# A two-layer model kernel: loads, table, TensorE and step order of the lead-in changed

## The chip, the cores and the metric

The kernel runs on one core of a Trainium2 chip. The metric is the device time of one execution in microseconds (us). A core has the engines PE (TensorE, matmuls and transposes), DVE (VectorE), ACT (ScalarE), POOL (GpSimd) and SP (SyncE), each with its own instruction queue that is worked off in order. DMA loads are issued from the queues of SP, ACT and POOL.

## The reference, cut to what matters

All numbers are float32. There are 2 x 1024 tokens of 256 channels, in 16 tiles of 128 tokens. Layer 0 normalizes the rows, runs grouped attention over 16 query heads of 16 channels with rotary positions, and gates its result with a feed-forward network whose weights are entries of a table of 16 numbers. Layer 1 does the same with a recurrent attention and a mixture of eight experts.

```
xn = layernorm(x)
s  = attention(xn)                       # q, k, v, rope, softmax, W_O
g  = silu(down(silu(gate(xn)) * up(xn))) # weights lut[idx]
x  = x + s * g
xn = layernorm(x)
s  = recurrent_attention(xn, Wx, Ww, bw, Wk, Wv, Wr, Wout, gamma, beta)
g  = silu(shared_experts(xn) + top_2_of_8_experts(xn))
x  = x + s * g
```

The change touches the start of layer 0 above all: layer norm, q, k, v, the first scores.

## The kernel before

The kernel is cut into small steps, and a step is a Python function that issues a few instructions on several engines. The string `ORDER` (L78 to L100), 1982 letters long, says in which order the steps are issued: each letter takes the next step of its kind. No scheduler moves anything afterwards, so the string sets the order of every engine's queue and, for DMA loads that a step issues, of the load queues as well. Semaphores hold an instruction until its operands are there.

Steps of layer 0 that the text speaks of, with the letter in front:

- `a`, `stats(t)`, for two tiles of tokens: two `bn_stats` and two `bn_aggr` on DVE, a root on ACT (L162), a reciprocal on DVE (L163) and, for the first sequence (tiles 0 to 7), a product on DVE (L167). At tile 8 it also clears the second sequence's buffers on POOL.
- `b`, `norm(t)`: one tile normalized, on ACT (L179) in the first sequence and on DVE (L181) in the second.
- `e`, `turn_x(t)`: four transposes on PE (L189) for two tiles, and one copy on ACT (L192).
- `f`, `qkv(t)`: one 128x512 product on PE over two halves of the channels (L200), the rotary products `cs` on DVE (L205), the values' copy on ACT (L211).
- `g`, `rotate(t)`: four operations on POOL (L223, L226) which finish q and k.
- `h`, `turn_k(t)` and `j`, `l`, turns of q: transposes on PE (L237, L269, L279) and a copy on ACT each.
- `m`, `largest`: one score product `mx` of 32 rows by 512 on PE (L291) and its maximum on DVE (L298), 512 times.
- `w`, `weigh`: the score product `sc` (L314, L322) and its exponential on ACT (L326), 512 times. `v`, `gather`: the weighted values `cx` (L339, L350).
- `z`, `decode`: one of 16 rounds over one of 8 pieces of the feed-forward weights on POOL (L252, L256). The first round of a piece issues its `idx` load on SP (L248).
- `W`: the product of two decay weights from `fold`, which lies in the buffer of `s_sb` (L603). `A`: gate, up and down products of layer 0 (L539, L555).
- From `>` on come the steps of layer 1; among them `r` (recurrence), `o` (routing), `F X G H D S` (experts), `k u U` (collecting and writing out).

Ahead of the steps stand the loads: x in seven pieces, taken in turn by SP and ACT; `cst` (identity and other constants), `lut` and `wo` on POOL; `wqkv`, `rope` and, last, `fold` on ACT. PSUM is one pool of eight banks of 128x512 in layer 0.

Of the kernel before, what the change touches and what calls it, by code (L numbers as in the profile page):

```python
# [12 lines left out]
F32 = mybir.dt.float32  # L13
I32 = mybir.dt.int32
AF = mybir.ActivationFunctionType
# [3 lines left out]
P = 128  # L19
# [3 lines left out]
NTC = NT // P  # L23
CPB = S // P
E = 256
KC = E // P
XLOADS = ((0, 1), (1, 2), (2, 4), (4, 6), (6, 8), (8, 12), (12, 16))
NBLK = NT // 512
BC = 512 // P
EPS = 1e-5  # L30
# [45 lines left out]


ORDER = """  # L78
aaabbbabeazbebfgefgfgbzbbbfgehfgeffghgfjfhmmgmhmmgmmmmmmjfmmmlWmwmzmmwwwmmwlmmwmmwzmwwmwmmzwmmwm
wmwwmwmmmmljmmmzzwwmmvmmzmwvmzwmmmmlvmmmmvmmwwzwmwmzmwmwmwzmwmwgmzwmwwmmmmlvvazmwmmmwzwbvvmwzwmw  # L80
mwmmwmwmwmwjbmwzwmmmzzwweyhwmmwmmwmvwmzmmvzwwmmfmwwmvwmwgmmwwzavwmmmmwwvvwmwlvazvwmmmmwwfmmwwwwm
jzmmmwwzmwwmwzwmmmwzwmwvmwgmmmwzwvmwmwmwwmwmwwmzmmmlyvwmmmvmwwmvwmzwmvbwzmmzwvwzmmbwvwwmmwwmmhez
wwmmjmwwmbmmwwvwwmmvmmwwwwmvmmwmwwwvwwwmmmlfyjwwbmzwvzmwzmwvwwmmvmwwmvwwmmwmmwfmwwmeywwmmzwmzzmw
mwwzmgwzzmmfmmmmwmwvvwwmmzzwwvmmgmwwwmvwmmzwmvwmmwvmmwgmlfwwwmzvwzwmmvwmwmzmmwwjywmmwwzmmwgwmmmz
wzhwmwwwmmzvwmwmwmmvvwwzwzmmmwvmwmwwmwvmmzwmjlvwzwzmwmmwvmwwwmmmzvhwwmwmzmwzzzzzwmmwmwwzmmwwmmww
mwmmvwwzmwzmmvwzmwwmwmvwmmmwzwzwvylwwmmwmzvmmmwwwvmmmmwwwzvvzwmwzzmzmzwmwjmzwwmmwzwwywmwzwmwmmvm
zzwmzmppzjvzzmmzwwwwwvzmwwzwlvmwmmvwmwwmwvmmmwwwzmvvwmmwwmwzmqmmwwwwmmqwwmzmwmzzwmvmmwwvwwmmmmmv
vmmmwwzmpylwwmmwmvwmwwmmwvwzwwwwzmmzvwwwmmwzmvwmmmmwwwqpwmmwwmwzmzjwmmmmwmmpqmmwwvvwmmwjpvmzwwmv
wwwwqzy<pzqlwzmwmvmwmwmwwvmwmmwmwvwmwmwmvmwmwmwmwqmwmwzwmwwmwmmwmmwmwpwmwmmwmvvwmmmwmmvwwwmvzvzw
mmmzAAmwwmjlymwwmmzmmvwmmmwwvzzzvmwmmwwmwmwmwwwmmwwwmwvwwwwwwmvvwmwmmwmAwmmwAmmzwwyAzlmwwmAjmmmw  # L90
AAmmmwvzvwwwmmmwvmwmmmzwwvwwmmmwmvwzwwmmmwmvwmwmmwwvwwwwvzwwwwvvzwwmmqylmwmwvwmmwvwwmwwmmvmzwmmw
wwmmwmwwwwmwmwmwyAmmmmAmmmmAzjmwwwvvmmwmzvmmwwvwmwmwmmvlmwwwmmwvwwwwmmwzvwwwwmmmvmwwmmmwwwmwmwww
mmmwwmmmwmwmwvwmmwvvmwwmwmmvzwmwwwwzylvwzwwwwwwvvwwwwvvwwwwvwwwwyAvvwwwwApwwwwAAqwwwwvvwwwwpAvvp
AqypAqAqAApAApqpAAqqpAAq>nniAAAnAAAiAAAAniAiAnoiAiAnoAAoAnAnrrrAAoiAnAAoArAsAAcAAAiAcnonArncsAii
nrsoincr)onssnrosooossoosoocioiooorsocoocsoosooooroooioooooooooiioooorroooiooorroorrr]FXFFciXFiG
GXrHcXGiFHXFFGDFSrHXFDHGciXrDDcSGXrHHcGDFSGXXFSDFSHGrHSXFDHGSXGcDrHDXFFDcSHGGSFSXFDHXiHGrDSXFDHr
FrDSSGXGrrHXrFrFSrHDGXGcXDSHGFHGSDXrFSFHDXDcGHGXDiHXFFGirSHGFSiDHSDcSXDSHrFXDcFGrcSGXHFiHXGDGSFX
DHXrcSHDGXDGHFFXGHXSGDFXSrHcDFHGGSFXSXFrSDDHGSHDGSFSXDHrrHiGXSDDrFGXHrrSSrDrHSGDrHcDSSckrdkkuukU
ukrdkUkucUurciUkkiuUUkurckduUrcdcurUkukUkuUrrUdukurUkrduUUuuUU
"""  # L100


def attention(nc, tc, st, b0, small, singles, xs, xnT, s_sb, wlut, ident, epst, wqkv_d, rope_d, lut_d, idx_d, wo_d):

# [2 lines left out]
    att = st.enter_context(tc.tile_pool(name="att", bufs=1))  # L109
# [4 lines left out]

    wqkv = att.tile([P, KC, 512], F32, name="wqkv")
    nc.scalar.dma_start(wqkv, wqkv_d)
    rope = att.tile([P, 2, CPB, 8], F32, name="rope")
    nc.scalar.dma_start(rope, rope_d)
    lut = att.tile([P, LUT], F32, name="lut")
    nc.gpsimd.dma_start(lut, lut_d)  # L120
    wo = att.tile([P, KC, E], F32, name="wo")
    nc.gpsimd.dma_start(wo, wo_d)


    knat = [att.tile([P, KV, SLOT], F32, name=f"knat{k}") for k in range(4)]
# [12 lines left out]
    def clear(b):  # L138
        nc.gpsimd.memset(vpads[b][:, :, :, HD : HD + 1], 1.0)
        nc.gpsimd.memset(vpads[b][:, :, 0, 0 : SLOT - HP], 0.0)  # L140
        nc.gpsimd.memset(vpf[b][:, NV * HP :], 0.0)
        for T in range(NQT):
            nc.gpsimd.memset(qns[b][:, T, :, :, HD:], 0.0)

    clear(0)

    def values(b, c, k):
        at = (c * KV + k) * HP
        return vpf[b][:, at : at + SLOT]


    mvs, rstds = {}, {}

    def stats(t):

        mv = att.tile([P, 2, 2], F32, name=f"mv_a{t}")
        for k in range(2):
            bst = att2.tile([P, 6], F32, tag="bst", name=f"bst_a{t + k}", bufs=4)
            nc.vector.bn_stats(bst, xs[:, t + k, :])
            nc.vector.bn_aggr(mv[:, k, :], bst)  # L160
        rstd = att.tile([P, 2], F32, name=f"rstd_a{t}")
        nc.scalar.activation(rstd, mv[:, :, 1], AF.Sqrt, bias=epst)  # L162
        nc.vector.reciprocal(rstd, rstd)  # L163
        if t == CPB:
            clear(1)
        if t < CPB:
            nc.vector.scalar_tensor_tensor(  # L167
                mv[:, :, 0], mv[:, :, 0], -1.0, rstd, ALU.mult, ALU.mult
            )
        for k in range(2):  # L170
            mvs[t + k] = mv[:, k, 0:1]
            rstds[t + k] = rstd[:, k : k + 1]
# [224 lines left out]
    def each(f, *ranges):  # L397
        return [lambda a=a: f(*a) for a in itertools.product(*ranges)]

    return {  # L400
        "a": each(stats, range(0, NTC, 2)),
        "b": each(norm, range(NTC)),
        "e": each(turn_x, range(0, NTC, 2)),
        "f": each(qkv, range(NTC)),
# [15 lines left out]
def two_layer_kernel(  # L420
# [22 lines left out]
    nc = tc.nc  # L443
    ctx.enter_context(tc.manual_schedule())
    pers = ctx.enter_context(tc.tile_pool(name="pers", bufs=1))
    small = ctx.enter_context(tc.tile_pool(name="small", bufs=2))
# [14 lines left out]
    xs = pers.tile([P, NTC, E], F32, name="xs")  # L461
    x_v = x_d.rearrange("(c p) e -> p c e", p=P)
    for n, (lo, hi) in enumerate(XLOADS):
        (nc.sync, nc.scalar)[n % 2].dma_start(xs[:, lo:hi, :], x_v[:, lo:hi, :])
    cst = pers.tile([P, C_ALL], F32, name="cst")
    nc.gpsimd.dma_start(cst, cst_d)
    ident = cst[:, C_ID : C_ID + P]
    before = cst[:, C_BEF : C_BEF + P]
    cols = cst[:, C_COL : C_COL + P]
# [3 lines left out]
    epst = pers.tile([P, 1], F32, name="epst")  # L473
    nc.vector.memset(epst, EPS)
    xnT = pers.tile([P, KC, NT], F32, name="xnT")
    s_sb = pers.tile([P, NTC, E], F32, name="s_sb")
    wxw = pers.tile([P, KC, E], F32, name="wxw")

# [19 lines left out]
    singles = []  # L498
    ffw = ctx.enter_context(ExitStack())
    wpool = ffw.enter_context(tc.tile_pool(name="ffw", bufs=1, side="right"))  # L500
    wlut = wpool.tile([P, WLUT], F32, name="wlut")
# [49 lines left out]
    def down0(n, k):  # L551
# [19 lines left out]
    b0 = seq0.enter_context(tc.tile_pool(name="b0", bufs=1, side="right"))  # L571
    att = ExitStack()
    singles.append(att.enter_context(tc.tile_pool(name="one", bufs=8, space=psum)))
    steps = attention(
        nc, tc, att, b0, small, singles, xs, xnT, s_sb, wlut, ident, epst,
        wqkv_d, rope_d, lut_d, idx_d, wo_d,
    )

    def end_sequence0():
# [6 lines left out]
    def go(last):  # L586
        for letter in order:
            if letter == last:
                break
            steps[letter].pop(0)()  # L590


    fold = s_sb.rearrange("p c e -> p (c e)")[:, 0 : 2 * KC * E].rearrange(
        "p (k f d) -> p k f d", k=KC, d=E
    )
    nc.scalar.dma_start(fold, fold_d)

    def weights_of_decays():
        ps = bank1("wxwp")
# [755 lines left out]
    def each(f, *ranges):  # L1355
        return [lambda a=a: f(*a) for a in itertools.product(*ranges)]
# [150 lines left out]
```

## Time and profile before

| | |
|---|---|
| median of 3 runs | 985.89 us (985.19 to 987.99) |
| profiled execution | 988.5 us, its span 986.7 us |
| busy: PE, DVE, ACT, POOL | 950.2, 631.3, 533.9, 587.9 us |
| first matmul on PE | 11.08 us after the span's start |
| first `mx` | 34.88 us |
| last decoding on POOL | about 493 us |

Times in a timeline count from the span's start. "x4" is a count of instructions; PE records a float32 product as two matmuls. PE counts as busy while any matmul is in flight, so a busy PE can still be at less than its best. In a line of the waits, the engine and line in front waited for the one behind the arrow.

### The profile page before, as it was taken

The numbers are of one execution on the slowest core, as the hardware profiler recorded it, in microseconds if no ns is written. First come the engines' busy times: TensorE is split into PE (matmuls) and PEld (weight loads), VectorE is DVE, ScalarE is ACT, GpSimd is POOL, SyncE is SP. The second block draws the span as 40 slices with busy tenths as digits, with TensorE's granted clock in tenths as the row PEclk, the third lists the DMA queues.
The fourth block names the chain that finished last, engine by engine and source line by source line (L and its number), as shares of the span: only waits on it lengthen the run. The fifth ranks groups of instructions, "written<-read, shape, count | busy, mean of one in ns | idle before, by whom it ended". The sixth has DMA issues, their size and how long they took to land.

```text
span 986.7 us, 17241 instructions
## 1 busy us (share of the span) xinstructions
PE 950.2 (96%) x6708; PEld 519.8 (53%) x6708; DVE 631.3 (64%) x1226; ACT 533.9 (54%) x1007; POOL 587.9 (60%) x483
## 2 busy tenths in 40 slices
PE   5999999999999999999999999999999999999965
PEld 2587343333433434333345474756457777767754
DVE  4799887877878767676770132767776625631893
ACT  3347766556665666677578535326433453563131
POOL 6999999999999999999901120302002454454232
PEclk9999999999999999999999999999999999999988
DMA  5000000000000000000000040102600122121242
GB/s 173 2 2 13 2 1 12 2 12 2 12 1 2 12 1 12 2 1 1 1 1 1 1 137 4 44 1 68 195 1 28 54 66 65 58 77 55 73 137 70
DMA packets 17960, 34.53 MB, mean 35 GB/s; under 512 B 2877, under 2 KB 11343, under 8 KB 17535
## 3 DMA queue, kind: packets, MB, share of 16 engines
q1 hardware_dynamic: 12583, 20.65, 6.5%
q0 software_dynamic: 3920, 10.74, 3.5%
q10 hardware_dynamic: 1376, 2.03, 0.6%
q8 instruction: 54, 0.88, 0.4%
q14 instruction: 27, 0.22, 0.1%
HBM read 22.01 MB, written 11.40 MB: 34 GB/s over the span
## 4 chain that ended last, share of the span: by engine, by line
PE 88%; DVE 6%; DMA 2%; ACT 1%; issue 1%; POOL 1%; POOLq 0%; ACTq 0%; SPq 0%; DVEq 0%
PE sc L322 14%; PE mx L291 14%; PE cx L350 12%; PE gu L539 7%; PE gus L723 4%; PE d L555 4%; PE gue L963 4%; PE dne L991 3%; PE qkv L200 3%; PE lev L1201 2%; DVE top L298 2%; PE so L392 2%; PE sc L314 1%; PE s L1324 1%; PE kp L1105 1%; PE rp L1105 1%
## 5 line engine op out<-in xcount | busy, mean ns | idle before, releaser
L298 DVE TENSOR_REDUCE top<-mx 128x1 f32<-128x512 f32 x512 | 324.8, 683 | 91.9 <-PE mx L291 64.2
L326 ACT ACTIVATE e<-sc 128x512 f32<-128x512 f32 x512 | 272.8, 600 | 130.1 <-PE sc L322 61.0
L291 PE MATMUL mx<-kT,qTa 32*128 32x512 f32 x1024 | 279.4, 625 | 0.0
L252 POOL TENSOR_SCALAR pick<-idx,lut 128x544 f32<-128x544 int32 x120 | 252.3, 2102 | 11.2
L322 PE MATMUL sc<-qTb,kT 32*128 32x512 f32 x960 | 258.3, 625 | 0.0
L256 POOL TENSOR_TENSOR wlut<-wlut,pick 128x544 f32<-128x544 f32 x120 | 160.8, 1340 | 10.0
L291 PEld LDWEIGHTS mx<-kT,qTa 32*128 32x128 f32 x1024 | 102.1, 183 | 66.5 <-DVE top L298 28.3
L322 PEld LDWEIGHTS sc<-qTb,kT 32*128 32x128 f32 x960 | 89.8, 183 | 79.9 <-DVE top L298 28.1
L350 PE MATMUL cx<-e,vpad 128*32 128x512 f32 x960 | 123.5, 602 | 0.0
L565 POOL TENSOR_TENSOR sgt<-s_sb,g 128x256 f32<-128x256 f32 x16 | 13.1, 816 | 158.2 <-ACT g L563 158.2
L936 POOL DMA_INDIRECT xg<-xn_h,who x39 | 39.7, 1017 | 102.4 <-ACT s_sb L1331 71.4
L1004 POOL DMA_INDIRECT y_h<-ye,who x39 | 39.9, 1023 | 63.0 <-ACT ye L999 16.9
L539 PE MATMUL gu<-xnT,wlut 128*128 128x512 f32 x160 | 73.3, 598 | 0.0
L350 PEld LDWEIGHTS cx<-e,vpad 128*32 128x32 f32 x960 | 21.1, 108 | 83.0 <-issue 71.6
L549 DVE TENSOR_TENSOR h<-sg,gu 128x512 f32<-128x512 f32 x20 | 13.8, 688 | 70.9 <-ACT sg L548 54.8
L975 DVE TENSOR_TENSOR sge<-sge,gue 128x176 f32<-128x176 f32 x39 | 13.1, 338 | 62.9 <-ACT sge L974 62.7
L963 PE MATMUL gue<-wgu,xT 128*128 x156 | 52.3, 460 | 0.6 <-DVE w L1239 0.6
L539 PEld LDWEIGHTS gu<-xnT,wlut 128*128 128x128 f32 x160 | 29.0, 190 | 33.7 <-issue 29.5
L555 PE MATMUL d<-wlut,h 128*128 128x256 f32 x192 | 43.6, 381 | 0.5 <-ACT s_sb L395 0.5
L723 PE MATMUL gus<-xnT,wgs 128*128 128x512 f32 (+1 forms) x96 | 43.4, 598 | 0.5 <-ACT aT L1116 0.5
L1208 DVE TENSOR_TENSOR rd<-rd,up 128x512 f32<-128x512 f32 x48 | 33.2, 733 | 16.1 <-PE lev L1201 16.0
L555 PEld LDWEIGHTS d<-wlut,h 128*128 128x128 f32 x192 | 36.0, 190 | 8.7 <-issue 2.7
(226 smaller groups left out, 1349.7 us busy)
## 6 DMA issues: line engine op xcount, KB each, us to landing
xn_h<-xn SPq DMA_DIRECT2D x16, 256.0 KB, 3.3
yk<-y_h SPq DMA_DIRECT2D x16, 256.0 KB, 2.9
wgu<-in_wgu SPq DMA_DIRECT2D x1, 2816.0 KB, 9.9
idx<-in_idx SPq DMA_DIRECT2D x8, 272.0 KB, 2.7
out_x<-g SPq DMA_DIRECT2D x16, 128.0 KB, 1.7
wd<-in_wd SPq DMA_DIRECT2D x1, 1408.0 KB
w<-in_w SPq DMA_DIRECT2D x1, 1024.0 KB
wgs<-in_wgs SPq DMA_DIRECT2D x1, 704.0 KB
```

Source lines behind the costliest of these rows:

```text
L252: nc.gpsimd.tensor_scalar(dst, codes[piece], float(j), lut[:, j : j + 1], ALU.is_equal, ALU.mult)
L256: nc.gpsimd.tensor_tensor(wlut[:, at], wlut[:, at], dst, ALU.add)
L291: nc.tensor.matmul(ps, qTs["qTa", g, c // BC][at, ts(c % BC, P)], kTs[b][at, T // 2, ts(half, 512)], start=True, stop=True,)
L298: nc.vector.tensor_reduce(tops[g, c][:, half, i : i + 1], ps, AX.X, ALU.max)
L322: nc.tensor.matmul(ps, kTs[b][at, T // 2, ts(c, P)], qTs["qTb", g, h][at, :], start=True, stop=True)
L326: nc.scalar.activation(e, ps, AF.Exp, scale=1.0 / math.sqrt(E))
L350: nc.tensor.matmul(cxs[g, h][SLOT * i : SLOT * (i + 1), :], values(b, c, 4 * (T // 2) + i), es.pop((n, i)), start=(c == 0), stop=(c == CPB ...
L539: nc.tensor.matmul(hT0[which], wlut[:, lo + kc * P :][:, 0:P], xnT[:, kc, ts(n, 512)], start=(kc == 0), stop=(kc == KC - 1),)
L555: nc.tensor.matmul(po[:, 0:E], hidden(n)[:, f, ts(k, P)], wd0[:, f, :], start=(f == 0), stop=(f == NF0 - 1),)
L723: nc.tensor.matmul(ps[:sz, which, :], wgs[:, kc, which * SH_CH + lo : which * SH_CH + lo + sz], xnT[:, kc, ts(n, 512)], start=(kc == 0), s ...
L963: nc.tensor.matmul(ps[:, 0 : 2 * EI], xT[:, kc, :], late["gu"][:, kc, bass.ds(e * (2 * EI), 2 * EI)], start=(kc == 0), stop=(kc == KC - 1),)
L1004: nc.gpsimd.indirect_dma_start(out=y_h[:, :], out_offset=bass.IndirectOffsetOnAxis(ap=who[:, i : i + 1], axis=0), in_=tiles.pop(("y", i))[ ...
```

## The change

- The loads of x for tiles 8 to 15 and of `fold` no longer stand in front. They are issued on SP from the third `scales` step; a small DVE write into those tiles of x, in the same step, is what the loads of x wait for. Of `cst` only the identity is loaded at first; the rest and `wo` follow on POOL after the first clearing of buffers. `rope` goes from ACT's queue to POOL's. Of the five pieces of x left, ACT issues one and SP four.
- ACT takes one root of a constant right after its two load issues, which brings its table.
- `stats` ends with the root. The reciprocal and the product are a step of their own, `scales`, letter `t`.
- PE multiplies a zeroed part of `xnT` with itself four times into four banks that nobody reads, at the very start. DVE writes the zeros.
- `ORDER` is another string, of 1990 letters: the eight `t` are new, all other letters are as many as before. Its start:

```
before aaabbbabeazbebfgefgfgbzbbbfgehfgeffghgfjfhmmgmhmmgmmmmmmjfmmmlWmwmz
after  atbbazeatbbtafbetgfgbafegtbbbfhgbfegffgjhfemgmgmzmhhazWmmmmmmmjfltfm
```

Counted in the string before, letters 298 to 459 are the same in both (eight places later in the new one), and nearly the same up to about letter 930. After that the two differ all the way to the end.

```diff
-XLOADS = ((0, 1), (1, 2), (2, 4), (4, 6), (6, 8), (8, 12), (12, 16))
+XLOADS = ((0, 1), (1, 2), (2, 4), (4, 6), (6, 8))
...
     wqkv = att.tile([P, KC, 512], F32, name="wqkv")
     nc.scalar.dma_start(wqkv, wqkv_d)
+    nc.scalar.activation(att.tile([P, 1], F32, name="root"), epst, AF.Sqrt)
     rope = att.tile([P, 2, CPB, 8], F32, name="rope")
-    nc.scalar.dma_start(rope, rope_d)
+    nc.gpsimd.dma_start(rope, rope_d)
...
-    nc.gpsimd.dma_start(wo, wo_d)
+    for k in range(4):
+        nc.tensor.matmul(bank(f"none_{k}"), xnT[:, 0, 0:P], xnT[:, 0, 0:512], start=True, stop=True)
...
     clear(0)
+    late_loads(0)
+    nc.gpsimd.dma_start(wo, wo_d)
...
         nc.scalar.activation(rstd, mv[:, :, 1], AF.Sqrt, bias=epst)
-        nc.vector.reciprocal(rstd, rstd)
         if t == CPB:
             clear(1)
+        mvs[t], rstds[t] = mv, rstd
+
+    def scales(t):
+        mv, rstd = mvs[t], rstds[t]
+        nc.vector.reciprocal(rstd, rstd)
+        if t == BC:
+            nc.vector.memset(xs[:, CPB:, 0:1], 0.0)
+            late_loads(1)
         if t < CPB:
             nc.vector.scalar_tensor_tensor(
...
-        (nc.sync, nc.scalar)[n % 2].dma_start(xs[:, lo:hi, :], x_v[:, lo:hi, :])
+        (nc.sync, nc.scalar)[n == 1].dma_start(xs[:, lo:hi, :], x_v[:, lo:hi, :])
...
-    nc.gpsimd.dma_start(cst, cst_d)
+    nc.gpsimd.dma_start(cst[:, 0:P], cst_d[:, 0:P])
...
+    nc.vector.memset(xnT[:, 0, 0:512], 0.0)
...
+    def late_loads(part):
+        if part == 0:
+            nc.gpsimd.dma_start(cst[:, P:], cst_d[:, P:])
+            return
+        for lo in range(CPB, NTC, 4):
+            nc.sync.dma_start(xs[:, lo : lo + 4, :], x_v[:, lo : lo + 4, :])
+        nc.sync.dma_start(fold, fold_d)
...
-    nc.scalar.dma_start(fold, fold_d)
```

More of the change, by code (lines that the diff above doesn't have):

```diff
@@ L78 @@
 ORDER = """
[L79 to L99, printed above, removed]
-"""
-def attention(nc, tc, st, b0, small, singles, xs, xnT, s_sb, wlut, ident, epst, wqkv_d, rope_d, lut_d, idx_d, wo_d):
+atbbazeatbbtafbetgfgbafegtbbbfhgbfegffgjhfemgmgmzmhhazWmmmmmmmjfltfmmmmwmwwmmwmwmmwmmmlwmmmwzwmw
@@ new lines @@
+wmwmmmgwzlmmwmmwmwwmwmmwmwmzmgwzvmmmmvvbmmmwmmwjlmwzmzmzwbwmwmmwmzwzvmmmwmmzwvmzmmmvemmwlmmmmmwm
+vvwmwmwmwmwmwwmwmmwwmwhmmwwmmwvwmmwvwwmmmwjzzmzwmwwwmvzwmmmwwzmazvfvwmmzwmtzwwvvalymtwgmmfzmwwzz
+wvmmmwjwwmwmwmmwwmwmwzwmmmwzwmwvmwgmmmwzwvmwmwmwwmwmwwmzmmmlyvwmmmvmwwmvwmzwmvbwzmmzwvwzmmbwvwwm
+mwwmmhezwwmmjmwwmbmmwwvwwmmvmmwwwwmvmmwmwwwvwwwmmmlfyjwwbmzwvzmwzmwvwwmmvmwwmvwwmmwmzmwfmwzwmeyw
+wmmwmzzmwmwwmgwzmmfmzmmmwmwvvwmwmwwvmzmmwwwgmvwmmzwmvwmmwvmmwgmlfwwwmzvwzwmmvwmzmwmzmwwjywmzmwzw
+mmwgwmmmzwhwmwwwmmvzwmwmwmmvvwwwzzmmmwvmwmwwmwvmmzwmjlvwzwzmwmmwvmwwwmmmzvhwwmwmzmwzzzzzwmmwmwwz
@@ new lines @@
+mmwwmmwwmwmmvwwzmwzmmvwzmwwmwmvwmmmwzwzwvylwwmmwmzvmmmwwwvmmmmwwwzvvzwmwzzmzmzwmwjmzwwmmwzwwywmw
+zwmwmmvmmzzwzmppzjvzzmmzwwwwwvzmwwzwlvmwmmvwmwwmwvmmmwwwzmvvmwwmmwwzmqmmwwwwmmqwwmzmwmzzwmvmmwwv
+wmmmmwmvvmmmwwzmpylwwmmwmvwmwwwmmvwzwwwwmmzvwwwmzmwzmvwmmmmwwwqpwmmwwmwzmzjwmzwmwmmwypqpwmmmwmmm
+vvqwmwmvzzmwmmmmjlqpwwwwwwmvvwmwwwwmvzwzzmmwvwwzmmvwzw<mmmwwmpqwwmmwwmmmwmwwwmmmwmwwzvvmmmwmmwvw
+mmmvwwwmjAmwmmlAwwmmvvwmwmwmmvymmmmmwvwwmwmmwmwwmwwmwwwmmwwwmmzwmwwmmmwwmwvvwwmmyzlAAwwmmzvmmwwv
+wwmwwmmvAmwmmvvwwwmvAAAwmmmwmwjwmmwmwmwwmwwwmmmwwmmmwmmzwwvvwwwmwwmvjwwwmvwmzzmmlyAzwwwmvmmwmzvA
@@ new lines @@
+mwwwwzmvvwwmmwwwmwwmmwmmwwwmmzwmmmmwwwwzvmmmmwwwvwmwwmmwvwwwmyAlmmmmvvmmwmqzwwmmvvmwwwmmmvmwwwmm
+mwzwmwzwmwwmwwmwwmwmwvmwmwwmwvwmzmmwmwvwzwwwzlyvvwwwwwwwvvvwwwwwwwwvAvAwwwwyApApqvwwwwvAwwwwvAAw
+wwwvwwwvAAvpqApAqyApAqpAqqpApqAq>nAnAnAAAAAiAAiAAniAnAAioAniiAnArrnriAAniAAAicAAAArAAAriAocAoion
+osAnAnonioinnorsnocsoio)oscsoorsosioosrooososooooroooosooococsooorooocooooooroooroioooiorr]FrrXr
+FFGcXXFFiHGXGrHXDFcGHFGSDXDXrHcHGDrcSFiFrFHSXDcGDGHXFrcSXGSXDFHFGHFGDHSDSXXrHDSSiGFcrXDGSHrrFFGX
+DHrrGSHFXDXDHSSrrFGDFXGHGSSrHXDDFicXGXrHGFXcSFSDrHHGSDGXiHDcFGiXFDHrSHFSXGDDGcFXSrHiFFScXDSGHGXD
@@ L109, in attention @@
+XFFHGSrcSHDGXrcFSHXDiHFGSXDrFGFXDHGSHDFSGXDHrSrHGXDXGDHFiXSGSSDHFirDHrFGXSDSrrSHGDXSrHGDSrHDSckc
+rckdkuukkuUrkUcduUruckiUkkuUkudrkcUdUurikurdUucUukkrkUurkUUuruUrduUuUU
+"""
+def attention(
+    nc, tc, st, b0, small, singles, xs, xnT, s_sb, wlut, ident, epst,
+    wqkv_d, rope_d, lut_d, idx_d, wo_d, late_loads,
+):
     att = st.enter_context(tc.tile_pool(name="att", bufs=1))
@@ L401, in attention @@
         "a": each(stats, range(0, NTC, 2)),
+        "t": each(scales, range(0, NTC, 2)),
         "b": each(norm, range(NTC)),
@@ L573, in two_layer_kernel @@
     singles.append(att.enter_context(tc.tile_pool(name="one", bufs=8, space=psum)))
+    fold = s_sb.rearrange("p c e -> p (c e)")[:, 0 : 2 * KC * E].rearrange(
+        "p (k f d) -> p k f d", k=KC, d=E
+    )
+    def late_loads(part):
[5 more added lines that the diff above has]
+        nc.sync.dma_start(fold, fold_d)
     steps = attention(
         nc, tc, att, b0, small, singles, xs, xnT, s_sb, wlut, ident, epst,
-        wqkv_d, rope_d, lut_d, idx_d, wo_d,
+        wqkv_d, rope_d, lut_d, idx_d, wo_d, late_loads,
     )
@@ L590, in go @@
             steps[letter].pop(0)()
[L593 to L596, printed above, removed]
     def weights_of_decays():
```

## The prediction

> **What bounds the kernel now.** I read the page's slices first, then the chain's shares by engine, then time windows, then the timeline of the first 45 us, where all of the change but the order lies.
>
> ```profile
> PE   5999999999999999999999999999999999999965
> ...
> DVE  4799887877878767676770132767776625631893
> ...
> POOL 6999999999999999999901120302002454454232
> PEclk9999999999999999999999999999999999999988
> ...
> PE 88%; DVE 6%; DMA 2%; ACT 1%; issue 1%; POOL 1%; POOLq 0%; ACTq 0%; SPq 0%; DVEq 0%
> ```
>
> TensorE (PE) is busy in all slices but the first and the last two, and the chain of waits is 88% PE. So time saved before PE gets going should move everything behind it, unless another engine takes over. The windows say which other engine is near:
>
> ```profile
> 40.00:60.00 20.00, 19.95 (x201) 16.06 (x201) 19.66 (x34) 12.29 (x23) 18.97 (x12) 1.00 0.00 1
> ...
> 80.00:100.00 20.00, 19.40 (x246) 11.87 (x245) 18.17 (x36) 16.14 (x28) 19.18 (x12) 1.00 0.06 16
> ...
> 160.00:180.00 20.00, 20.00 (x139) 6.83 (x138) 13.66 (x24) 11.80 (x23) 18.99 (x12) 1.00 0.00 1
> ...
> 480.00:500.00 20.00, 20.00 (x156) 6.54 (x148) 12.80 (x23) 13.93 (x27) 12.81 (x8) 1.00 0.00 1
> ...
> 940.00:960.00 20.00, 13.90 (x96) 10.95 (x94) 19.22 (x32) 6.10 (x12) 7.71 (x9) 0.90 0.33 108
> ```
>
> After the two times the columns are PE, weight load, DVE, ACT, POOL. VectorE (DVE) is full from 35 to 100 us (19.66 of 20), PE from there to 880, DVE again near the end. GpSimd (POOL) is some 95% busy until 493 with the decoding of the weights. The timeline of the lead-in:
>
> ```profile
> 4.97 0.34 ACTq L596 DMA_DIRECT2D s_sb<-in_fold  x1
> 5.33 1.28 ACT L162 ACT_TABLE_LOAD   x1 [5.33 <-DMA xs<-in_x]
> 6.63 0.30 ACT L162 ACTIVATE rstd_a<-mv_a,epst 128x2 f32<-128x2 f32 x1
> ...
> 10.44 1.57 ACT L179 ACTIVATE xn<-xs,mv_a,rstd_a 128x256 f32<-128x256 f32 x3
> ...
> 11.08 1.60 PE L189 MATMUL xnTp<-cst,xn 128*128 128x128 f32 x5 [11.08 <-ACT xn L179]
> ...
> 13.58 3.62 PE L200 MATMUL qkv<-wqkv,xnT 128*128 128x512 f32 x4
> ...
> 14.41 2.12 POOL L252 TENSOR_SCALAR wlut<-idx,lut 128x544 f32<-128x544 int32 x1 [5.38 <-DMA idx<-in_idx]
> ...
> 17.64 5.32 PE L200 MATMUL qkv<-wqkv,xnT 128*128 128x512 f32 x12
> ...
> 34.88 1.13 PE L291 MATMUL mx<-kT,qTa 32*128 32x512 f32 x6
> ```
>
> PE does nothing for 11.08 us. The first root waits for ACT's table, and the table for ACT's own issue of the `fold` load (4.97 to 5.31), though its statistics are there at 4.52. Then three pairs' roots go ahead of the first `norm` (10.44). The first four qkv matmuls (a float32 product is recorded as two) take 3.62 us, those from 17.64 on 0.43 to 0.44 each: PE begins at half speed. The loads are late too:
>
> ```profile
> idx<-in_idx SPq DMA_DIRECT2D x2, 272.0 KB, 10.2
> ...
> wqkv<-in_wqkv ACTq DMA_DIRECT2D x1, 512.0 KB, 10.5
> ```
>
> `wqkv`, issued at 2.2, lands near 12.7; the first matmul on it is at 13.5.
>
> **The change, part by part.** *Loads.* 1 MB of x (tiles 8 to 15), 512 KB of `fold`, 256 KB of `wo` and 168 KB of `cst` leave the front. ACT issues 128 + 512 KB instead of 2.0 MB, SP 896 KB before the first 272 KB of `idx`, POOL 136 KB and then the 424 KB of the late `cst` and `wo`. Before, the windows show 205, 336 and 314 GB/s in the first three stretches of 5 us. With ACT and SP sharing evenly, ACT's 640 KB are through when 1.4 to 1.8 MB have moved: 6.5 to 8 us for `wqkv`, and about 9 for `idx`. SP waits at the third `scales` for a DVE memset; behind it stand only x 8 to 15, `fold` and the second piece of `idx`. I have the memset at 9.6, x 8 to 11 at about 13 (512 KB at some 350 GB/s, and about the 1.7 us from issue to landing that the page has for a 128 KB `out_x`), and `stats(8)` on DVE at 14: just covered. If it is late, `cs` of tile 2 is behind it and each us costs one. `fold` is wanted at some 30 us: free.
>
> *ACT's table.* ACT is through with its issues at 1.8, so the table (1.28) and a root of `epst` lie in time in which ACT has nothing to do. The first real root moves from 6.63 to 4.55. The Trainium skill, page "ScalarE: Activation LUTs", section "What ACT_TABLE_LOAD costs", wants a further 1.38 us of drain at a switch; the trace has the root 1.30 after the load's start. By the page the table would be ready at 4.5, by the trace at 3.1: at or before 4.55, so the sum is the same.
>
> *Zeros on TensorE.* Four 128x512 products, eight recorded matmuls, after a DVE memset of 128x512 (the memsets of 128x1 and 128x128 took 59 and 165 ns: about 0.49), so from 1.4 us on. Row: before, PE began at 11.1 and ran at half speed until about 17.0, 5.9 us. The skill, page "TensorE: Matmul & The Clock Gate", section "What's actually happening", says that the array starts at half clock and is let up after one busy window of 3.4 us which runs free: 3.4 to 6.8 us here. It speaks against a part of this: zeros that outlast the first norms stand in front of the real work. By the row seven are slow (0.86) and one fast: they end at 7.8; by the rule between 6.5 and 8.3. Real transposes would be ready at 6.4. So the zeros cost about 1.4 us (0.1 to 1.9) and buy full speed from the first transpose on. What that is worth in the trace: four qkv matmuls 3.62 to 1.72, and 8 transposes at some 0.3 to 0.15: 3 us at most. The profile's granted clock reads 1.00 in the half-speed stretch; only the durations show it. I take the row.
>
> *The new lead-in walked by hand*, each step with its row of before: pair of statistics 1.17, root 0.30, reciprocal and product 0.36, norm 0.52, four transposes 0.60, qkv 1.72, eviction of a bank 0.59, `cs` 0.96, values 0.27, rotation 1.43; orders as the program issues them.
> - Norms 0 and 1: 5.3 to 6.3 (before 10.4 to 11.5). Transposes 7.8 to 8.4 (before from 11.1). qkv(0) 9.1 to 10.8.
> - ACT is then the queue in front: root, norms 2 and 3 and the second eviction end at 13.2; qkv(1), (2) 11.4 to 15.0; qkv(3) 15.6 to 17.3; qkv(4) to 19.7, (5) to 22.0, (6) to 23.7, turns of q and k, qkv(7) to 26.7, transposes 8.
> - First `mx` at 27.3, against 34.88. But before had then done one more qkv (1.72) and one more turn of k (0.6): PE is 5.3 us ahead.
> - DVE is full from `cs` of tile 7 on, at 26.7; before from that of tile 8, at 34.61. Less one `cs` (0.96) it is 7.0 us ahead; the sixth pair of statistics, done early, is only moved.
> - POOL: the clearing of the second sequence's buffers (2.4 us, idle time before) now stands between two rotations, and decoding starts at about 9 instead of 14.41. Rotation 7 ends at 29.1; one rotation and one decoding pair (3.44) later it is where it was at 37.1: 3.1 us ahead.
>
> Root and scaling as two steps add no instruction; they let DVE do other statistics while ACT takes the root. Of the two DVE memsets the large one (0.49) lies ahead of data, the other costs DVE some 0.07. `rope` and `wo` on POOL's queue cost issue time of 0.6 each, ahead of its first decode, which waits for `idx` anyway; without that cover, 0.6.
>
> What is late next? DVE sets the pace from 35 to 100 us, PE's lead is 5.3: I take 6.0. POOL's smaller lead should not bind:
>
> ```profile
> POOL knat L223 <- DVE cs L205: 0.9, 1, 0.9
> ```
>
> That is all it waited between 40 and 500 us, so it is full, but its users are far behind: rotations of tiles 9, 11 and 13 end at 74.7, 131.1 and 197.5, their k is turned at about 97, 154 and 223; decoding ends at 493, the first down projection is at 527.
>
> *Order of the rest.* From the 306th to the 460th letter the orders agree, and nearly so to the 930th; then they part. By count: two adjacent steps on the same 32 rows of PE 15 before, 14 after; ACT table loads 55 and 56; last ten recurrence steps behind the first `collect` in both. PE's idle time outside the lead-in is some 25 us (986.7 - 950.2 - 11.4), 16 of them in 880 to 980. A better order can win perhaps 5 of these, a worse one lose as much or a little more. I take 0, for the counts agree.
>
> Sum against the profiled execution: 988.5 (span 986.7) - 6.0 = 982.5. It stood 2.6 above the median of the runs (985.89), so on that scale 985.9 - 6.0 = 979.9.
>
> **The rivals.** *A: the lead is eaten.* A load is late (x 8 to 11 behind its memset, or `wqkv` or `idx` in the shared queues), or PE goes back to half speed in the gaps of ACT's queue, and 3 to 5 of 6 us go. For: ACT and DVE have no slack between 9 and 16. Against: bytes in front fall by 1.9 MB. It gives 983 to 985.
> *B: slower, by the new order in the attention.* Late in the attention eight recorded sc matmuls, which take four groups of 32 rows in turn, need 1.14 us, eight of qkv with all rows some 3.45: they run beside each other. I suppose that two neighbours in the same rows can't; such a collision leaves PE busy but costs up to 0.86, two recorded matmuls of 0.43. Place: the parted stretch, 330 to 527 us. It decides when some ten such collisions or equal waits are added (9 us): 985.9 - 6 + 9 = 989. Repeats at a distance of two or three are 177 before, 181 after, which speaks against it.
> *C: the order gains as well,* in the stalls of the last 100 us: 985.9 - 6 - 5 = 975.
> That the change does not do what it says: if zeros do not lift the clock, the transposes still start near 8.4 instead of 11.1, and half speed costs the 3 us: 983, in A.
>
> **How the numbers follow.** Forecast 0.60 (its own range 977 to 983), A 0.17, B 0.13, C 0.10. A measurement of this kernel tells about 0.3% from no change, 3.0 us, so faster means under 982.9. Faster: most of the forecast and all of C, 0.67; same: A and the forecast's upper edge, 0.20; slower: B, 0.13. The range of 8 in 10 runs from C's middle to just short of B's: 974.5 to 988.
>
> **What would show it.** Right: a table load on ACT near 1.8; first real root near 4.6; PE busy from about 1.4, real transposes at 7 to 8.5 at 0.15 each; first `mx` at 26 to 29; decoding over near 490; down projections some 6 us earlier. Wrong: L200 matmuls of 0.86 after 9 us, DVE waiting for x at 14, PE waiting for `wqkv`, or a first `mx` at 27 with the end of attention not moved: then the order took it.

## The result and the profile after

| | before | after |
|---|---|---|
| median of 5 runs | 985.89 us (985.19 to 987.99) | 980.91 us (979.61 to 981.83) |
| profiled execution, its span | 988.5, 986.7 us | 980.9, 979.0 us |
| first `mx`, start | 34.88 us | 26.56 us |
| first `sc` of 512 columns (L322, after L340) | 83.7 us | 78.5 us |
| last turn of k | 245.9 us | 240.4 us |
| first product of W_O | 303.8 us | 297.1 us |
| first down projection of layer 0 | 527.7 us | 520.0 us |
| first gate or up product of the experts | 763.6 us | 752.8 us |
| last product of the recurrence (L1324, after L1351) | 972.1 us | 964.3 us |

The ratio is 0.9944, 95% interval 0.9929 to 0.9958: 5.5 us less, 4.1 to 7.0 (the two medians are 5.0 apart). All rows but the first two are starts on PE. The lead is there at the first `mx` (8.3 us, less 2.35 us of PE work that the new order does later: 6.0) and stays: it is between 5 and 11 us in every later row, and 7.8 in the last. The last three rows lie where the two orders differ, so they compare two orders as well as two leads; `head_only` below has the old order there. Two more runs of before left its median and range as they were. The profiled executions differ by more than the medians, because that of before lay 2.6 us above its median.

The page of the changed kernel: the slices, then the chain's shares by engine.

```profile
PE   8999999999999999999999999999999999999974
...
DVE  5898887887767767765760134466877635721993
...
POOL 7999999999999999999902020202002355453243
PEclk9999999999999999999999999999999999999998
...
PE 91%; DVE 5%; issue 1%; DMA 1%; POOL 1%; ACT 0%; POOLq 0%; SPq 0%; ACTq 0%; DVEq 0%
```

The first digit of PE is 8 instead of 5, and DMA has gone from 2% of the chain to 1%. Nothing else in the picture moved: PE bounds the kernel as it did. The windows say the same (columns PE, weight load, DVE, ACT, POOL):

```profile
40.00:60.00 20.00, 20.00 (x295) 17.56 (x294) 19.64 (x36) 11.85 (x23) 19.08 (x17) 1.00 0.01 2
...
940.00:960.00 20.00, 16.10 (x163) 13.27 (x159) 17.73 (x38) 7.36 (x16) 9.30 (x11) 0.91 0.48 149
```

DVE is as full in the first as before (19.64, before 19.66). The timeline of the lead-in, where the lead is made:

```profile
1.49 5.71 PE L130 MATMUL none<-xnT 128*128 128x512 f32 x8 [1.49 <-DVE xnT L495]
1.67 1.28 ACT L121 ACT_TABLE_LOAD   x1 [1.67 <-PEq L1524]
...
4.62 0.29 ACT L172 ACTIVATE rstd_a<-mv_a,epst 128x2 f32<-128x2 f32 x1 [1.45 <-DVE mv_a L170]
...
5.34 1.09 ACT L197 ACTIVATE xn<-xs,mv_a,rstd_a 128x256 f32<-128x256 f32 x2 [0.43 <-DVE mv_a L185]
...
7.03 0.43 DVE L169 BATCH_NORM_STATS2 bst_a<-xs 128x6 f32<-128x256 f32 x1 [1.72 <-DMA xs<-in_x]
7.04 0.60 PE L207 MATMUL xnTp<-cst,xn 128*128 128x128 f32 x4
...
9.05 1.98 PE L218 MATMUL qkv<-wqkv,xnT 128*128 128x512 f32 x4 [1.41 <-ACT xnT L210]
9.27 2.15 POOL L270 TENSOR_SCALAR wlut<-idx,lut 128x544 f32<-128x544 int32 x1 [1.55 <-DMA idx<-in_idx]
...
14.11 0.42 DVE L169 BATCH_NORM_STATS2 bst_a<-xs 128x6 f32<-128x256 f32 x1
...
26.56 1.14 PE L309 MATMUL mx<-kT,qTa 32*128 32x512 f32 x8
```

The root waits for its own statistics (L170) alone, the first norms (L197) start at 5.34 instead of 10.44, and decoding at 9.27 instead of 14.41. The first four recorded qkv matmuls take 1.98 in place of 3.62. `stats(8)` at 14.11 shows no wait for the late x. The second pair of statistics (7.03) waited 1.72 us for its own part of x; in the runs below that have the same first loads these statistics start at 5.8 to 6.0. So this one execution was late there by about 1 us, and the first `mx` of single profiles scatters by some 0.8 us for that alone (25.8 in `no_root`). From the DMA issues of the lead-in (the last number is us from issue to landing):

```profile
idx<-in_idx SPq DMA_DIRECT2D x2, 272.0 KB, 6.2
...
wqkv<-in_wqkv ACTq DMA_DIRECT2D x1, 512.0 KB, 5.6
```

`wqkv`, issued at 1.18, lands at 6.8 instead of 12.7; no matmul waits for it.

### The profile page after: what moved, and what is told of

Its sections match the earlier page's. It is cut to its first block, busy times and chain, and to the rows that moved or that the text cites. A ratio compares the mean times of both kernels' runs of the same rounds, so it can differ in the third digit from the quotient of the medians.

```text
span 979.0 us, 17252 instructions
## 1 busy us (share of the span) xinstructions
PE 953.0 (97%) x6716; PEld 522.4 (53%) x6716; DVE 627.9 (64%) x1228; ACT 533.8 (55%) x1009; POOL 586.7 (60%) x485
## 4 chain that ended last, share of the span: by engine, by line
PE 91%; DVE 5%; issue 1%; DMA 1%; POOL 1%; ACT 0%; POOLq 0%; SPq 0%; ACTq 0%; DVEq 0%
PE sc L340 15%; PE mx L309 14%; PE cx L368 12%; PE gu L559 7%; PE gue L990 5%; PE d L575 4%; PE gus L750 4%; PE dne L1018 3%; PE qkv L218 3%; PE lev L1228 3%; PE sc L332 2%; PE rp L1132 1%; PE so L410 1%; PE vp L1159 1%; PE kp L1132 1%; PE ap L1132 1%
## 5 line engine op out<-in xcount | busy, mean ns | idle before, releaser
L309 PE MATMUL mx<-kT,qTa 32*128 32x512 f32 x1024 | 287.0, 626 | 0.4 <-DVE top L316 0.4
L340 PE MATMUL sc<-qTb,kT 32*128 32x512 f32 x960 | 257.5, 625 | 0.5 <-DVE top L316 0.5
L309 PEld LDWEIGHTS mx<-kT,qTa 32*128 32x128 f32 x1024 | 102.5, 183 | 66.1 <-DVE top L316 27.3
L340 PEld LDWEIGHTS sc<-qTb,kT 32*128 32x128 f32 x960 | 93.2, 183 | 79.3 <-DVE top L316 26.4
L1031 POOL DMA_INDIRECT y_h<-ye,who x39 | 39.9, 1024 | 69.2 <-ACT ye L1026 25.4
L1018 PE MATMUL dne<-wd,hTe 88*128 x156 | 40.0, 380 | 0.5 <-ACT hTe L1011 0.5
```

The source lines that it names most:

```text
L309: nc.tensor.matmul(ps, qTs["qTa", g, c // BC][at, ts(c % BC, P)], kTs[b][at, T // 2, ts(half, 512)], start=True, stop=True,)
L340: nc.tensor.matmul(ps, kTs[b][at, T // 2, ts(c, P)], qTs["qTb", g, h][at, :], start=True, stop=True)
L1018: nc.tensor.matmul(ps[:, 0:E], hT[:, k, :], late["d"][:, k, bass.ds(e * E, E)], start=(k == 0), stop=(k == 1),)
```

## The experiments

The theory: the lead is made in the lead-in and passed on whole, the order of the rest is worth nothing. Each part of the change was then taken out or done alone. Each ratio is to the kernel before on the same chip, with its 95% interval; starts are those of one profiled execution.

**Head and tail of the order.** `head_only` is the whole change with the old letters from the 335th on, `tail_only` the kernel before with the new letters from its 327th on.

```diff
 # head_only
-ORDER = new
+ORDER = new[:334] + old[326:]
 # tail_only
-ORDER = old
+ORDER = old[:326] + new[334:]
```

> All of the change, but behind letter 334 of the order the old letters follow (both strings have used the same steps by then). Theory: the lead-in carries the whole gain and the rest of the order is worth nothing: 979 to 982.5, the first mx at 26.6, and a lead of 5 to 7 us over the kernel before kept to the end. Rival: the new order of the rest has a share of its own: if it gained 2 us or more, this kernel is at 983 or above; if it cost 2 us or more, this one is at 979 or below.

> The kernel before with the new letters from letter 327 on, and nothing else of the change. Theory: 985 to 987.5, within 0.15% of before, with the first mx at 34.9. Rival, the rest of the order has a share of its own: at or below 984 if it gains, at or above 988 if it costs.

`head_only` took 980.87 us, ratio 0.9943 (0.993 to 0.9957), the same as the full change; first `mx` at 26.4, first product of W_O at 296.9. So 1656 letters in another order are worth nothing beside the new head, to within some 2 us. As its rest has the old order, its starts compare with before's one to one: 6.0 us ahead at the first down projection (521.7), 6.0 at the first experts product (757.6). `tail_only` took 988.58 us, ratio 1.0023 (1.0013 to 1.0032): beside the old head the same letters cost 2.3 us. That is outside my 985 to 987.5; the rival, a share of its own that costs, holds. Its first product of W_O is still at 303.0 and its first down projection at 527.5, as before; its last down projection starts at 681.5 (before 678.5). Why they cost something there and not behind the new head was not separated and stays open.

**No zeros on TensorE.**

```diff
-    for k in range(4):
-        nc.tensor.matmul(bank(f"none_{k}"), ...)
...
-    nc.vector.memset(xnT[:, 0, 0:512], 0.0)
```

> The changed kernel without the four products of zeros and without the write of zeros. Theory: PE begins at about 6.5 with 8 transposes at half speed (0.3 each), qkv(0) and qkv(1) take 3.5 each instead of 2.0 and 1.9, first mx at 28.5 to 29.5 instead of 26.6, and the time rises by 2 to 3 us to 983 to 984. Rival: ACT's queue is what sets the pace there (its second root waits for x until 8.2), the half speed lies in gaps of PE, first mx within 0.8 us of 26.6 and the time within 1 us of 980.9.

982.51 us, ratio 0.9964 (0.9951 to 0.9978): 1.6 us more than the change by the medians, 2.0 by the ratios, at the lower edge of the 2 to 3 expected. Its timeline:

```profile
6.38 1.09 PE L205 MATMUL xnTp<-cst,xn 128*128 128x128 f32 x4 [6.38 <-ACT xn L195]
...
8.14 3.78 PE L216 MATMUL qkv<-wqkv,xnT 128*128 128x512 f32 x4 [0.67 <-ACT xnT L208]
```

The transposes start 0.66 us earlier than behind the zeros but take 1.09 instead of 0.60, and qkv(0) takes 3.78 instead of 1.98. The first `mx` is at 28.5, 1.9 us later, and every milestone behind it is 1.9 to 2.0 later: W_O 299.1, the first experts product 754.7, the recurrence's last product 966.2. This is the plainest evidence that time saved in the lead-in goes one to one to the end. It has its limit: the profile of `no_root` below is 0.76 us ahead of the change's at the first `mx` and 0.15 at the first down projection, a drift that spreads evenly over the 500 us between.

**The late loads issued at once.**

```diff
     wo = att.tile(...)
+    late_loads(0)
+    nc.gpsimd.dma_start(wo, wo_d)
+    late_loads(1)
...
-    late_loads(0)
-    nc.gpsimd.dma_start(wo, wo_d)
...
-        if t == BC:
-            nc.vector.memset(xs[:, CPB:, 0:1], 0.0)
-            late_loads(1)
```

> The changed kernel with its late loads issued at the start, on the same queues: rest of cst and wo directly behind lut on POOL, x 8 to 15 and fold on SP behind x 0 to 7 and ahead of the first piece of idx; no write in front of them. Theory: holding back is worth little where PE is concerned, since ACT's own two loads share the engines evenly with SP: wqkv lands below 9 us; idx lands at 12 to 13.5 instead of 9.3, decoding starts there, first mx within 1 us of 26.6, time within 1.2 us of 980.9. Rival: the 1.9 MB held back are the gain: wqkv past 10 us, first mx at 29 or later, time at 983 or above.

984.56 us, ratio 0.9985 (0.9977 to 0.9993): 3.7 us more than the change, first `mx` at 30.1. My theory (within 1.2 us) fell. But not `wqkv` is late: it lands 5.0 us after its issue, sooner than in the change. It is `idx`, now behind 1.5 MB on SP's queue, and POOL works off its own queue in order:

```profile
14.57 2.12 POOL L267 TENSOR_SCALAR wlut<-idx,lut 128x544 f32<-128x544 int32 x1 [6.79 <-DMA idx<-in_idx]
...
16.67 0.31 POOL L238 TENSOR_TENSOR knat<-cs 128x64 f32<-128x64 f32 x1
```

POOL waits 6.79 us at its first decode, and all rotations stand behind that: the first starts at 16.67 instead of 12.12. Decoding itself was in no hurry; what made it dear is that the new order puts it ahead of the first rotation. This is read from the timeline. A kernel with `idx` ahead of late loads that are issued at once was not run, so whether holding back x is worth anything beyond the place of `idx` stays open.

**No early root.**

```diff
-    nc.scalar.activation(att.tile([P, 1], F32, name="root"), epst, AF.Sqrt)
```

> The changed kernel without the early root of a constant on ACT. Theory: a table load does not wait for the data of the root behind it, only for ACT to be through with its issues of loads; it still runs at about 1.7, first real root still near 4.6, first mx within 0.5 us of 26.6, time within 1 us of 980.9, so the root itself bought nothing and the gain came from taking loads off ACT's queue. Rival: the load goes with its root, from 4.6 to 5.9, everything behind is 1.3 us later: 982.2.

980.38 us, ratio 0.9943 (0.993 to 0.9957): nothing is lost.

```profile
1.67 1.28 ACT L171 ACT_TABLE_LOAD   x1 [1.67 <-PEq L1523]
...
4.61 0.29 ACT L171 ACTIVATE rstd_a<-mv_a,epst 128x2 f32<-128x2 f32 x1 [1.65 <-DVE mv_a L169]
...
6.01 0.43 DVE L168 BATCH_NORM_STATS2 bst_a<-xs 128x6 f32<-128x256 f32 x1 [0.71 <-DMA xs<-in_x]
...
8.04 1.98 PE L217 MATMUL qkv<-wqkv,xnT 128*128 128x512 f32 x4 [0.81 <-ACT xnT L209]
```

The table load stands in ACT's queue ahead of the real root and does not wait for that root's statistics. Before, it started at 5.33 only because ACT was still issuing loads until 5.31. So emptying ACT's queue of loads is what brought the root forward, and the root of a constant did nothing. The two lower lines show the change's order with x in time: statistics at 6.01 instead of 7.03, qkv(0) at 8.04 instead of 9.05, first `mx` at 25.8.

**Root and scaling joined.** Each `t` stands directly behind its `a`.

```diff
-ORDER = "atbbazeatbbtafbetgfg...
+ORDER = "atbbatzeatbbatfbegfg...
```

> The changed kernel with each scales step directly behind its stats step, as in the kernel before; all else in the new order. Theory: DVE waits for ACT's root between the pairs, the third pair's statistics end some 0.8 us later, ACT's third root stands ahead of norms 2 and 3, so first mx is 0.5 to 1 us later and the time 981.4 to 982. Rival: the split is worth nothing, since x for the second pair lands at about 6 to 7 anyway: first mx within 0.3 us, time within 0.6 us of 980.9.

981.01 us, ratio 0.9951 (0.9938 to 0.9965), first `mx` at 26.8: 0.2 later than in the change, whose x came late, and 1.0 later than in `no_root`, whose x came in time as here (5.89). So the theory may be right about the lead-in. In time the split is worth nothing that can be measured: the intervals of the two ratios overlap, and half a us is below what they tell.

**All but the order.** The edits with the old string; `t` directly behind each `a`.

> All of the change but the order: the old string, with each scales step directly behind its stats. Theory: the first norm again waits for the third pair's root, so the first transposes are at 10 to 10.5 instead of 7.0 and PE has stood idle for 3 us after its zeros; the first mx lies at 31.5 to 33.5 (34.9 before; this order has one qkv and one turn of k more ahead of it, 2.35 us), time 982.5 to 985. Rival: loads, table and zeros carry all of it whatever the order: first mx at 29, time at 981.5 or below. Other rival: without the order nothing is left: 985.5 or above.

985.55 us, ratio 0.9996 (0.9988 to 1.0004): nothing is left of the gain. I had expected part of it. The timeline shows four things at once:

```profile
1.50 6.03 PE L130 MATMUL none<-xnT 128*128 128x512 f32 x8 [1.50 <-DVE xnT L495]
...
9.88 1.61 PE L207 MATMUL xnTp<-cst,xn 128*128 128x128 f32 x5 [2.36 <-ACT xn L197]
...
12.38 3.62 PE L218 MATMUL qkv<-wqkv,xnT 128*128 128x512 f32 x4
...
13.51 0.43 DVE L169 BATCH_NORM_STATS2 bst_a<-xs 128x6 f32<-128x256 f32 x1 [1.98 <-DMA xs<-in_x]
...
17.14 2.12 POOL L270 TENSOR_SCALAR wlut<-idx,lut 128x544 f32<-128x544 int32 x1 [7.03 <-DMA idx<-in_idx]
```

The first norm comes behind three pairs' roots, at 9.24, so PE stands still for 2.36 us behind the zeros and is at half speed again. `stats(8)` comes ahead of norm 3 in this order and waits 1.98 us for the x that is now loaded late. And `idx`, issued behind the late loads, comes at 17.1. The next runs take these apart.

**The order alone.** The kernel before with the new string without its `t`, its rest included.

> The kernel before with the new order of all steps (without its t, so stats and scales stay one step) and nothing else of the change. Theory: order and loads work only together. Here wqkv still lands near 12.7 and the first idx at 14.4, and POOL decodes ahead of its rotations, so the first mx is at 30 to 31.5 (without any lead it would be at 34.9 less the 2.35 us of PE work that this order puts off: 32.5) and the time is 984 to 985.5. Rival: the order alone is the gain, since old_order had none: first mx at 28 or less, 982.5 or below. Other rival: neither does anything alone: 985.5 or above.

(This kernel, `old_bridge`, `old_mended` and `better3` ran on another chip, on which the kernel before took 998.99 us; the extra 13 us lie behind the first experts product. Only ratios and times ahead of it are compared.) Ratio 1.0013 (1.0001 to 1.0025), a little slower, and the last of the three outcomes that I had named; first `mx` at 32.3 (30 to 31.5 expected), which is before's 34.9 less the 2.35 us of PE work that the new order puts off.

```profile
5.29 1.28 ACT L162 ACT_TABLE_LOAD   x1 [5.29 <-DMA xs<-in_x]
...
12.19 3.75 PE L200 MATMUL qkv<-wqkv,xnT 128*128 128x512 f32 x4 [2.84 <-DMA wqkv<-in_wqkv]
...
14.49 2.12 POOL L252 TENSOR_SCALAR wlut<-idx,lut 128x544 f32<-128x544 int32 x1 [7.77 <-DMA idx<-in_idx]
```

The norms now come at 7.31 but the table is late, PE waits 2.84 us for `wqkv`, then runs at half speed, and `idx` holds POOL 7.77 us. The order opens a path that the loads do not let it use. The loss may come from the rest of the string, which cost 2.3 us in `tail_only`; the new head with the old loads and the old rest was not run.

**Bridging the gap, and `idx` first, with the old order.** `old_bridge` is `old_order` with seven zero products; `old_mended` also loads the first piece of `idx` ahead of the late loads.

```diff
 # both
-    for k in range(4):
+    for k in range(7):
 # old_mended alone
+    load_codes(0)          # ahead of the first step
...
-        if j == 0:
+        if j == 0 and piece:
```

> The kernel old_order with seven products of zeros instead of four, so that PE is busy until its first transposes. Theory: in old_order PE stood idle from 7.5 to 9.9 and was back at half speed after 2.4 us; without the gap the first transposes are at about 10.1, all at full speed, and qkv(0) takes 2.0 instead of 3.6. But POOL's decode waits for idx until 17.1 there, so the first mx moves by less than 0.8 us and the time stays within 0.8 us of 985.5. Rival: PE's speed is what the old order lacks: first mx 1.5 to 2.5 us earlier, time 983 to 984. Against the theory of the gap: the first transposes are slow all the same.

> The kernel old_bridge with the first load of idx issued directly behind x 0 to 7 on SP, ahead of the late loads. Theory: with the old order the late loads stand in front of idx (decode at 17.1), and POOL's rotations stand behind that decode; with idx first, decoding starts at 8 to 9.5, the first mx is at 30.5 to 32 instead of 34.2, and 2 to 3.5 us of the gain come back: 982 to 983.5. Rival: the late first norm (9.2) sets it all: first mx past 33.2, time 984.5 or above.

`old_bridge`: ratio 0.9998 (0.9984 to 1.0011), first `mx` 34.3. Its timeline:

```profile
10.36 0.82 PE L207 MATMUL xnTp<-cst,xn 128*128 128x128 f32 x4 [0.16 <-ACT xn L197]
...
12.14 1.98 PE L218 MATMUL qkv<-wqkv,xnT 128*128 128x512 f32 x4
```

Full speed (1.98 in place of 3.62), and the first `mx` does not move. So the gap made the half speed, but that is not what the old order lacks. `old_mended`: ratio 0.9995 (0.9979 to 1.0011). Decoding starts at 10.2, and still the first `mx` is at 34.3; my theory that `idx` was the rest fell, and the rival's number (past 33.2) holds. What stands ahead of PE then:

```profile
13.62 0.43 DVE L169 BATCH_NORM_STATS2 bst_a<-xs 128x6 f32<-128x256 f32 x1 [2.20 <-DMA xs<-in_x]
...
14.83 0.29 ACT L172 ACTIVATE rstd_a<-mv_a,epst 128x2 f32<-128x2 f32 x1 [2.84 <-DVE mv_a L170]
15.03 0.58 ACT L197 ACTIVATE xn<-xs,mv_a,rstd_a 128x256 f32<-128x256 f32 x1
...
17.02 5.32 PE L218 MATMUL qkv<-wqkv,xnT 128*128 128x512 f32 x12
```

Norm 3 (15.03) is behind the root of tiles 8 and 9, which waits for the late x; PE's dense row of qkv starts at 17.02, and in before at 17.64. The old order and the held-back loads work against each other. That this chain alone sets the old order's first `mx` is read from the timeline; no run took it away.

**Two versions meant to be better.** `better` puts the second clearing of buffers back into POOL's idle time and the first copy of `xnT` ahead of the second root; `better3` is `better` with three zero products.

```diff
     nc.gpsimd.dma_start(wo, wo_d)
+    clear(1)
...
-        if t == CPB:
-            clear(1)
...
-ORDER = "atbbazeatbbt...
+ORDER = "atbbezaatbbt...
 # better3 alone
-    for k in range(4):
+    for k in range(3):
```

> The changed kernel with two edits. The clearing of the second sequence's buffers (2.4 us on POOL) goes back into POOL's idle time before its first decode, out of the row of rotations; and the first copy of turned x stands ahead of the second root on ACT. Theory: loads_at_once showed POOL's row of rotations on the path to the first mx, and cs of tile 7 waited 1.6 us for POOL in the changed kernel, so the first mx is at 25 to 26.2 and the time 979 to 980.4. Rival: PE's own row of qkv sets the first mx and DVE's wait is absorbed: first mx at 26.2 to 26.8, time within 0.6 us of 980.9.

> The kernel better with three products of zeros instead of four. Theory: the zeros end at about 6.0, ahead of the first norms (6.4), so real transposes start at 6.5 instead of 6.8; if PE is up to full speed by then the first mx is 0.2 to 0.4 us earlier than in better (25.6), 979 to 980. Rival: the half-speed time runs into the transposes and qkv(0) in part of the executions: first mx 0.5 to 1.5 us later, 980.5 to 981.5.

`better`: 979.97 us, ratio 0.9949 (0.9936 to 0.9963). Its first `mx` is at 25.6 and later starts are 1.0 us ahead of the change's (last turn of k 239.4, the recurrence's last product 963.3), but in time it cannot be told from the change (0.9944) or from `no_root`. The expected 25 to 26.2 was met by luck: x came in time here (5.96), and `no_root`, which has neither edit, is at 25.8. The wait of `cs` of tile 7 for POOL, which the first edit was to remove, is what it was in the change (1.63 us, at 26.28):

```profile
25.28 0.96 DVE L222 TENSOR_TENSOR cs<-qkv,rope 128x768 f32<-128x768 f32 x1 [1.64 <-POOL qn L243]
```

`better3`: ratio 0.9959 (0.9944 to 0.9974), first `mx` at 25.4, not told apart either. Its timeline:

```profile
1.49 5.32 PE L130 MATMUL none<-xnT 128*128 128x512 f32 x6 [1.49 <-DVE xnT L494]
...
6.65 0.60 PE L206 MATMUL xnTp<-cst,xn 128*128 128x128 f32 x4
```

Five of the six zero matmuls and part of the sixth run at half speed (starts 0.85 us apart; the transpose behind the last starts 0.73 after it) and the transposes at full: in this execution the zeros end just when they have done their work. Zeros needed up to 5.8 us in other runs (next section), so three products can be too few; the rival, half speed in part of the executions, was not tested.

## Why the prediction was right

The forecast was 979.9 us, the median is 980.91; the lead was put at 6.0 us and is 5.5 by the ratio, 5.0 by the medians.

- **PE bounds, so a lead-in gain passes on.** Right: `no_zeros` loses 1.9 us at the first `mx` and 1.9 at the recurrence's last product; `head_only` is 6.0 us ahead of before at the first down projection and at the first experts product.
- **The walk.** Norms 5.34 to 6.43 (said 5.3 to 6.3), `wqkv` landed at 6.8 (6.5 to 8), decoding at 9.27 (about 9), `stats(8)` at 14.11 (14, just covered), qkv(1) at 11.31 (11.4), `cs` of tile 7 at 26.28 (26.7). qkv(0) at 9.05 (9.1) is luck: two terms were off and cancelled. The zeros were over earlier, so the transposes ran from 7.04 to 7.64 (7.8 to 8.4); but the second pair of statistics, late by its load at 7.03, moved the second root to 8.23, ahead of the first copy, which cost PE 1.41 us of waiting at qkv(0). With x in time qkv(0) is at 8.04 (`no_root`). The first `mx` came at 26.56, not 27.3. Against before's 34.88 that is 8.3 us, less the 2.35 of work put off 6.0. The walk gave 5.3 for PE and 7.0 for DVE; the 6.0 in between was a judgement, and that it fits so well is in part luck too.
- **ACT's table.** The time was right (4.62 for the first real root, 4.55 said; no drain shows behind the load, as in the row of before: the root of a constant starts at 2.96, 1.29 after it), the cause only in part: the loads taken off ACT's queue did it, the early root nothing (`no_root`).
- **Zeros.** The sum said 3 us at most gained for about 1.4 of delay; `no_zeros` measures a net 1.6 to 2.0, and the delay was 0.66 (transposes at 7.04 against 6.38). The Trainium skill, page "TensorE: Matmul & The Clock Gate", section "What's actually happening", lets the array up after a free-running window of 3.4 us; from that the estimate was 3.4 to 6.8 us after the start. I had taken before's 5.9 us. The starts of the zero matmuls are 0.85 us apart at half speed and 0.43 at full, which dates the change: 3.0 us after the first in `old_mended`, 4.1 in the change, 4.7 in `old_order`, 5.8 in `loads_at_once`. The page's spread was the better guide than the one row of before, though the shortest lies under it. The estimate is for unbroken work: in `no_zeros`, where PE stood for 0.67 us between the transposes and qkv(0), half speed lasted 7.7 us, from 6.38 to 14.0.
- **"POOL's smaller lead should not bind."** It held in the change, where decoding was over at 488.7, 4.8 us earlier (the walk had POOL 3.1 ahead); yet not with room to spare: `loads_at_once` delays POOL's first rotation by 4.5 us and pays 3.5 at the first `mx`. Rival A should have been priced there, on `idx` in front of POOL's rotations.
- **Order of the rest at 0.** Right beside the new head (`head_only`); as a property of the order it was wrong, since beside the old head it costs 2.3 us.
- **What the forecast treated as a sum is not one.** It costed loads, zeros and order part by part. `old_order` (all but the order) gives 0, `order_only` gives a loss of 1.3 in 1000, together they give 5.5 us. As the timelines read, norms right behind their root pay only if table, `wqkv` and `idx` are early, and holding back x costs what it gains if `stats(8)` comes early in the order.
- **The rivals.** A (the lead is eaten) did not happen but was near: it is `loads_at_once`, 984.56 against its 983 to 985. B and C put 9 us of loss or 5 of gain in the order of the attention or of the last 100 us; `head_only`, equal to the change within some 2 us, excludes both.

## What to carry to other kernels

In a kernel that one engine bounds from its first busy stretch on, look at what that engine waits for in the first microseconds: a lead there was passed on whole here. Then trace each wait to the queue it stands in, not only to its operand: here a table load stood behind load issues, and rotations behind a decode whose table indices were late. Do not price an order of steps and an order of loads separately; test each without the other before believing either.

## What the runs showed of the hardware that was not expected

- A gap of 2.36 us on PE behind 6.0 us of work brought half speed back (`old_order`); one of 1.41 us did not (the change: 7.64 to 9.05). Two gaps in two kernels give no threshold. The Trainium skill's page "TensorE: Matmul & The Clock Gate" gives, in "What's actually happening", one idle window of about 3.4 us for it; the measured gap was shorter, and the measurement decides.
- The granted clock of the profile reads 1.00 in every half-speed stretch at the start of a kernel (before, `no_zeros`, the zeros), and only durations tell. The fall in `old_order` it does show: 0.96 from 5 to 10 us, 0.50 in the line below, 0.85 from 15 to 20 (the number after POOL).

```profile
10.00:15.00 5.00, 4.79 (x12) 2.47 (x12) 2.17 (x10) 2.35 (x7) 0.10 (x1) 0.50 0.83 269
```

- ACT's table load does not wait for the operands of the activation behind it (1.67 in `no_root`, with statistics ready at 4.6), but it does wait for load issues ahead of it on ACT (5.33 before, 5.29 in `order_only`; the last issue ends at 5.31 and 5.26).
- Products of zeros lift the speed as real ones do: transposes behind them take 0.60 for four, without them 1.09.
